# Attention over convolution projections: two halvings of v put off, transposes reordered at the image boundary, wider rows of v and a shifted k

## The chip, the cores and the metric

The kernel runs on one core of a Trainium2 chip. The metric is device time in microseconds, the median of several executions. "Span" is the time from the first to the last instruction of the one profiled execution. TensorE multiplies matrices; VectorE (DVE), ScalarE (ACT) and GpSimd (POOL) do the rest.

## The reference

Four images x of 64 x 64 x 256 in float32. Per image:

```python
q = einsum('bwhc,cd->bwhd', x, Wq) + bq      # 128 channels
k = einsum('bwhc,cd->bwhd', x, Wk) + bk      # 128 channels
v = einsum('bwhc,cd->bwhd', x, Wv) + bv      # 256 channels
pq, pk, pv = (t.reshape(B, -1, N) for t in (q, k, v))    # N = 4096
attention = softmax(einsum('bcn,bcm->bnm', pq, pk), axis=-1)
out = einsum('bcm,bnm->bcn', pv, attention)
return gamma * out.reshape(B, W, H, C) + x
```

## The kernel before

An image has two stages. In the first, 16 blocks of x are transposed, projected to q, k and v, and split into parts (h, l, d: "halving"). In the second, 128 units run: 16 groups of queries times 8 units of keys. A unit issues the energies of the unit three ahead, on TensorE, ScalarE takes exponentials, VectorE joins two of them, ScalarE and VectorE halve the product, and TensorE multiplies the halves of an earlier unit by the halves of v. The parts that matter:

```python
    vh = qkv.tile([P, NM, C + 2], F32R, tag="vh", name="vh")     # rows of 258 floats: 256 and two ones
    vl = qkv.tile([P, NM, C + 2], F32R, tag="vl", name="vl")
    vd = qkv.tile([P, NM, C], F32R, tag="vd", name="vd")
    # ... (cut)
    def project_v(b, i):
        images[b].v(i)
        v4 = now["v4"]
        m = slice(2 * i, 2 * i + 2)
        h = vh[:, m, :C]
        nc.scalar.activation(h, v4, AF.Identity, scale=UPPER * E)
        for t, f in ((vl, 1.0 / E), (vd, 1.0 / E + 1.0)):
            nc.vector.scalar_tensor_tensor(t[:, m, :C], h.bitcast(F32), -f, v4, ALU.mult, ALU.add)
    # energy(b, u, k): (cut)  weights are rows of k, the moving operand is q
        for to, f, first, last in ((sa, 0, True, False), (sa, 1, False, True), (sb, 2, True, True)):
            nc.tensor.matmul(to[:, i], kt[:, 2 * k + i, f, :], q[:, :, f, :], start=first, stop=last)
    # attend(b, u, j): (cut)  weights are h, l, d of the unit, the moving operand is a row of v
        for out_, left, right in ((a, h, vh), (a, l, vl), (bb[:, j, :], d, vd)):
            for i in range(4):
                nc.tensor.matmul(out_, left[:, i, n], right[:, m, :], ...)
    # the units of an image (cut)
        for u in range(STEPS):
            for k in range(2):
                if ahead < STEPS:
                    energy(b, ahead, k)
                if k == 0 and u + 2 < STEPS:
                    join(b, u + 2)
                    upper(b, u + 2)
            # ... (cut)
            halves(b, u + 1)
            # ... (cut)
            for j in range(NJ):
                attend(b, u, j)
        if b + 1 < B:
            images[b + 1].transposed(1)
            project_qk(b + 1, 0)
        while active:                  # the last output of the image
            proceed()
```

## Time and profile before

| | before |
|---|---|
| time | 2519.3 us (2519.1 to 2519.8, four runs) |
| TensorE busy | 2497.4 us, 99% of the span of 2516.5 |
| VectorE, ScalarE busy | 84%, 72% |
| granted clock of TensorE | 0.999 |

A TensorE that is busy for 99% of the span leaves two places to look: the 1%, and the pace of the matmuls within the 99%. The pace isn't in the durations, which overlap (282 ns is the mean of the sa matmuls of this trace), but in the starts. These two lines of the timeline of TensorE stand at the ends of the twelve energies of one unit in the steady stage (start us, duration us, instruction):

```profile
574.02 0.40 PE L311 MATMUL sa<-q,k 128*128 128x256 f32 x2
...
575.43 0.65 PE L359 MATMUL a<-vh,h 128*128 128x258 f32 x4
```

Twelve matmuls start in 1.41 us, 117.5 ns each, and this distance from start to start is the measure that the rest of the study uses.

### The profile page before, as it was taken

The numbers are of one execution on the slowest core, as the hardware profiler recorded it, in microseconds if no ns is written. First come the engines' busy times: TensorE is split into PE (matmuls) and PEld (weight loads), VectorE is DVE, ScalarE is ACT, GpSimd is POOL, SyncE is SP. The second block draws the span as 40 slices with busy tenths as digits, with TensorE's granted clock in tenths as the row PEclk, the third lists the DMA queues.
The fourth block names the chain that finished last, engine by engine and source line by source line (L and its number), as shares of the span: only waits on it lengthen the run. The fifth ranks groups of instructions, "written<-read, shape, count | busy, mean of one in ns | idle before, by whom it ended". The sixth has DMA issues, their size and how long they took to land.

```text
span 2516.5 us, 50017 instructions
## 1 busy us (share of the span) xinstructions
PE 2497.4 (99%) x19982; PEld 2455.1 (98%) x19982; DVE 2102.5 (84%) x2440; ACT 1806.1 (72%) x3138; POOL 424.6 (17%) x780
## 2 busy tenths in 40 slices
PE   9999999999999999999999999999999999999998
PEld 8999999999899999999989999999998999999998
DVE  5888888888688888888868888888886888888887
ACT  5777777776677777777667777777766777777775
POOL 4211111111411111111041111111114111111110
PEclk9999999999999999999999999999999999999999
DMA  7666666664766666666476666666648666666663
GB/s 238 214 192 210 198 203 197 193 207 147 236 214 189 206 198 201 201 191 205 138 243 220 194 192 207 200 206 194 190 143 254 213 197 195 201 200 206 198 191 108
DMA packets 137407, 498.92 MB, mean 198 GB/s; under 512 B 15536, under 2 KB 57264, under 8 KB 137168
## 3 DMA queue, kind: packets, MB, share of 16 engines
q0 software_dynamic: 92320, 453.17, 57.4%
q1 hardware_dynamic: 44304, 42.22, 5.6%
q8 instruction: 160, 2.62, 0.4%
q14 instruction: 79, 0.65, 0.1%
q10 hardware_dynamic: 544, 0.26, 0.0%
HBM read 445.25 MB, written 50.33 MB: 197 GB/s over the span
## 4 chain that ended last, share of the span: by engine, by line


## 5 line engine op out<-in xcount | busy, mean ns | idle before, releaser
L315 ACT ACTIVATE x<-sa 128x512 f32<-128x512 f32 x1024 | 609.5, 595 | 429.6 <-PE sa L311 367.6
L325 DVE TENSOR_TENSOR x<-x,y 128x1024 f32<-128x1024 f32 x512 | 625.4, 1222 | 172.9 <-ACT y L315 172.9
L311 PE MATMUL sa<-q,k 128*128 128x256 f32 x4096 | 759.2, 282 | 6.3 <-ACT x L315 6.0
L359 PE MATMUL a<-vh,h 128*128 128x258 f32 x4096 | 662.4, 284 | 0.0
L359 PE MATMUL a<-vl,l 128*128 128x258 f32 x4096 | 660.3, 283 | 0.0
L359 PE MATMUL bb<-vd,d 128*128 128x256 f32 x4096 | 651.9, 281 | 0.0
L311 PEld LDWEIGHTS sa<-q,k 128*128 128x128 f32 x4096 | 627.1, 188 | 8.0 <-ACT x L315 6.9
L336 DVE TENSOR_TENSOR l<-x,h 128x1024 fp32r<-128x1024 f32 x512 | 623.6, 1218 | 0.0
L339 DVE SCALAR_TENSOR_TENSOR d<-h,x 128x1024 fp32r<-128x1024 f32 x512 | 623.5, 1218 | 0.0
L315 ACT ACTIVATE y<-sb 128x512 f32<-128x512 f32 x1024 | 613.1, 599 | 0.0
L311 PE MATMUL sb<-q,k 128*128 128x256 f32 x2048 | 580.4, 283 | 0.0
L330 ACT ACTIVATE h<-x 128x1024 fp32r<-128x1024 f32 x512 | 543.5, 1061 | 34.9 <-DVE x L325 34.0
L359 PEld LDWEIGHTS a<-vl,l 128*128 128x128 f32 x4096 | 563.8, 189 | 0.0
L359 PEld LDWEIGHTS a<-vh,h 128*128 128x128 f32 x4096 | 561.5, 189 | 0.0
L359 PEld LDWEIGHTS bb<-vd,d 128*128 128x128 f32 x4096 | 557.6, 189 | 0.0
L295 POOL DMA_DIRECT2D k<-kf x512 | 279.7, 546 | 1508.1 <-PE sb L311 1476.0
L311 PEld LDWEIGHTS sb<-q,k 128*128 128x128 f32 x2048 | 385.4, 188 | 8.7 <-ACT y L315 0.8
L136 PE MATMUL qk<-wqk_sb,xts 128*128 128x256 f32 x512 | 121.5, 380 | 0.0
L157 PE MATMUL v<-xts,wv_sb 128*128 128x256 f32 x512 | 120.3, 379 | 0.0
L157 PEld LDWEIGHTS v<-xts,wv_sb 128*128 128x128 f32 x512 | 97.3, 190 | 13.2
L397 ACT ACTIVATE o<-o,r 128x256 f32<-128x256 f32 x126 | 57.4, 502 | 72.4 <-DVE r L380 72.4
L136 PEld LDWEIGHTS qk<-wqk_sb,xts 128*128 128x128 f32 x512 | 92.7, 191 | 10.1
(54 smaller groups left out, 884.5 us busy)
## 6 DMA issues: line engine op xcount, KB each, us to landing
k<-kf POOLq DMA_DIRECT2D x512, 768.0 KB, 4.8
x<-in_x_dram SPq DMA_DIRECT2D x128, 256.0 KB, 3.6
kf<-f POOLq DMA_DIRECT2D x64, 384.0 KB, 4.2
out_dram<-x POOLq DMA_DIRECT2D x63, 256.0 KB, 2.5
qd<-qks POOLq DMA_DIRECT2D x128, 64.0 KB, 2.9
qr<-qd SPq DMA_DIRECT2D x64, 128.0 KB, 3.1
wv_sb<-in_L_conv_Wv_dram POOLq DMA_DIRECT2D x1, 256.0 KB, 5.4
out_dram<-x SPq DMA_DIRECT2D x1, 256.0 KB, 3.9
```

The costliest lines, as they stand in the source:

```text
L136: nc.tensor.matmul(qk[:, s, :], self.xt[i][:, k, s, :], wqk_sb[:, k, :], start=(k == 0), stop=(k == KC - 1),)
L157: nc.tensor.matmul(vp[:, eh, :], wv_sb[:, k, eh * P : (eh + 1) * P], self.xt[i][:, k].rearrange("p s a -> p (s a)"), start=(k == 0), stop= ...
L295: nc.gpsimd.dma_start(t.rearrange("p (i s) f d -> p i s (f d)", s=2), kf[b, u % NU])
L311: nc.tensor.matmul(to[:, i], kt[:, 2 * k + i, f, :], q[:, :, f, :], start=first, stop=last)
L315: nc.scalar.activation(to[:, 2 * k : 2 * k + 2, :], sp.rearrange("p i j d -> p i (j d)"), AF.Exp, scale=scale,)
L325: nc.vector.tensor_tensor(x, x, y, ALU.mult)
L330: nc.scalar.activation(h, units[b, u], AF.Identity, scale=UPPER)
L336: nc.vector.tensor_tensor(l, x, h.bitcast(F32), ALU.subtract)
L339: nc.vector.scalar_tensor_tensor(d, h.bitcast(F32), 1.0 + E, x, ALU.mult, ALU.subtract)
L359: nc.tensor.matmul(out_, left[:, i, n], right[:, m, :], start=(t == i == 0 and (left is h or left is d and j == 0)), stop=(t == NU - 1 and ...
L397: nc.scalar.activation(o[:, j, :], o[:, j, :], AF.Identity, scale=r[:, j : j + 1])
```

## The change

Its intent: take work out of VectorE's queue where TensorE waits for it; let TensorE do the next image's transposes while the last output is scaled; and place two pairs of operands at other distances in memory. Nothing is computed differently. The core of the diff (cut; the guard's ok moves from its own 512 bytes to a y buffer, and ra into the tile of r, which frees the room):

```diff
+    VC = C + 4
-    ok = const.tile([P, B * NG * NJ], F32, name="ok")
-        vh = qkv.tile([P, NM, C + 2], F32R, tag="vh", name="vh")
-        vl = qkv.tile([P, NM, C + 2], F32R, tag="vl", name="vl")
+        vh = qkv.tile([P, NM, VC], F32R, tag="vh", name="vh")
+        vl = qkv.tile([P, NM, VC], F32R, tag="vl", name="vl")
@@ project_v
-            v4 = now["v4"]
+            units[b, "v4", i] = now["v4"]
+            if i < NI - 2:
+                halve_v(b, i)
@@ attend
-                        right[:, m, :],
+                        right[:, m, : out_.shape[1]],
@@ factors
-            r = work.tile([P, NJ], F32, tag="r", name=f"r_{b}_{g}")
+            r = work.tile([P, 2, NJ], F32, tag="r", name=f"r_{b}_{g}")
@@ finish_last
-            ra = work.tile([P, NJ], F32, tag="ra", name="ra", bufs=1)
@@ projections of the next image
                     pr.transposed(i + 1)
+                while i == 1 and active:
+                    proceed()
@@ units
+                if u in (1, 3):
+                    halve_v(b, NI - 2 + u // 2)
@@ end of an image
-            while active:
-                proceed()
```

More of the change, by code (lines that the diff above doesn't have):

```diff
@@ L209 @@
         ps_t = pool("ps_t", 1, space=PSUM)
-        vh = qkv.tile([P, NM, C + 2], F32R, tag="vh", name="vh")
-        vl = qkv.tile([P, NM, C + 2], F32R, tag="vl", name="vl")
+        vh = qkv.tile([P, NM, VC], F32R, tag="vh", name="vh")
+        vl = qkv.tile([P, NM, VC], F32R, tag="vl", name="vl")
         vd = qkv.tile([P, NM, C], F32R, tag="vd", name="vd")
         for t in (vh, vl):
-            nc.scalar.copy(t[:, :, C:], ones[:, : 2 * NM].rearrange("p (m t) -> p m t", t=2))
+            nc.scalar.copy(t[:, :, C : C + 2], ones[:, : 2 * NM].rearrange("p (m t) -> p m t", t=2))
         images, qd, kf, units, loads, now = [], {}, {}, {}, {}, {}
@@ L271, in project_v, with halve_v @@
             images[b].v(i)
-            v4 = now["v4"]
+            units[b, "v4", i] = now["v4"]
+            if i < NI - 2:
+                halve_v(b, i)
+        def halve_v(b, i):
+            v4 = units.pop((b, "v4", i))
             m = slice(2 * i, 2 * i + 2)
@@ L376, in factors @@
         def factors(b, g):
-            r = work.tile([P, NJ], F32, tag="r", name=f"r_{b}_{g}")
-            nc.vector.reciprocal(r, zall[:, b * NG + g, :])
-            nc.vector.tensor_tensor(r, r, gam.to_broadcast([P, NJ]), ALU.mult)
-            return r
+            r = work.tile([P, 2, NJ], F32, tag="r", name=f"r_{b}_{g}")
+            nc.vector.reciprocal(r[:, 0, :], zall[:, b * NG + g, :])
+            nc.vector.tensor_tensor(r[:, 0, :], r[:, 0, :], gam.to_broadcast([P, NJ]), ALU.mult)
+            return r[:, 0, :], r[:, 1, :]
         def whole(b, g):
@@ L394, in finish @@
             yield
-            r = factors(b, g)
+            r, _ = factors(b, g)
             for j in range(NJ):
@@ L414, in guard @@
             z = zall.rearrange("p n j -> p (n j)")
+            ok = ppool.tile([P, 4, NB], F32, tag="y", name="ok")[:, 0, : B * NG * NJ]
             nc.vector.tensor_scalar(ok, z, Z_LOW, None, ALU.is_ge)
@@ L429, in finish_last @@
             sums(b, g)
-            r = factors(b, g)
+            r, ra = factors(b, g)
             check = guard()
-            ra = work.tile([P, NJ], F32, tag="ra", name="ra", bufs=1)
             nc.vector.tensor_scalar(ra, r, 1.0 + E, None, ALU.mult)
```

## The prediction

> **What bounds the kernel now.** I read the page's head first: which engine is full, and at which clock.
>
> ```profile
> PE 2497.4 (99%) x19982; PEld 2455.1 (98%) x19982; DVE 2102.5 (84%) x2440; ACT 1806.1 (72%) x3138; POOL 424.6 (17%) x780
> PEclk9999999999999999999999999999999999999999
> ```
>
> TensorE is busy for 99% of the span at full clock. Nothing done on another engine can gain more than TensorE's own idle time plus any stretching of its matmuls. So I read the groups of instructions, for what fills it:
>
> ```profile
> L311 PE MATMUL sa<-q,k 128*128 128x256 f32 x4096 | 759.2, 282 | 6.3 <-ACT x L315 6.0
> L359 PE MATMUL a<-vh,h 128*128 128x258 f32 x4096 | 662.4, 284 | 0.0
> L359 PE MATMUL a<-vl,l 128*128 128x258 f32 x4096 | 660.3, 283 | 0.0
> L359 PE MATMUL bb<-vd,d 128*128 128x256 f32 x4096 | 651.9, 281 | 0.0
> ```
>
> Means of 281 to 284 ns are latencies of overlapping matmuls. What counts is the distance from one start to the next, which I took from the trace's start times (leaving out distances outside 100 to 140 ns, which are waits and changes of kind): 117.8 ns in the energies (sa and sb), 120.45 ns with vh, 120.55 with vl, 118.44 with vd. The 18432 such matmuls (6144 energies, 3 x 4096 for the output) make 6144 x 0.1178 + 4096 x (0.12045 + 0.12055 + 0.11844) = 2196 us, 87% of the span. Projections fill most of the rest, 216 ns for each of 1024 matmuls, 221 us.
>
> Then I searched the same start times for stalls of TensorE. The only repeated large one is at the second unit of each image. The timeline of TensorE there (second image):
>
> ```profile
> 703.29 0.40 PE L311 MATMUL sa<-q,k 128*128 128x256 f32 x2
> 703.53 0.28 PE L311 MATMUL sb<-q,k 128*128 128x256 f32 x1
> 703.64 0.40 PE L311 MATMUL sa<-q,k 128*128 128x256 f32 x2
> 703.88 0.28 PE L311 MATMUL sb<-q,k 128*128 128x256 f32 x1
> 705.71 0.50 PE L311 MATMUL sa<-q,k 128*128 128x256 f32 x2 [1.55 <-ACT x L315]
> 706.20 0.38 PE L311 MATMUL sb<-q,k 128*128 128x256 f32 x1
> ```
>
> The columns are start, duration, instruction, count, and in brackets idle time and its releaser. From 703.88 to 705.71 nothing starts, because the bank of sa is not read out yet. Why ScalarE is late, from its timeline and VectorE's:
>
> ```profile
> 701.13 0.59 ACT L315 ACTIVATE y<-sb 128x512 f32<-128x512 f32 x1
> 704.11 1.06 ACT L330 ACTIVATE h<-x 128x1024 fp32r<-128x1024 f32 x1 [2.39 <-DVE x L325]
> 705.08 0.58 ACT L315 ACTIVATE x<-sa 128x512 f32<-128x512 f32 x1
> ```
> ```profile
> 700.45 0.69 DVE L278 SCALAR_TENSOR_TENSOR vl<-vh,v 128x512 fp32r<-128x512 f32 x1
> 701.06 0.68 DVE L278 SCALAR_TENSOR_TENSOR vd<-vh,v 128x512 fp32r<-128x512 f32 x1
> 701.66 0.68 DVE L278 SCALAR_TENSOR_TENSOR vl<-vh,v 128x512 fp32r<-128x512 f32 x1
> 702.26 0.68 DVE L278 SCALAR_TENSOR_TENSOR vd<-vh,v 128x512 fp32r<-128x512 f32 x1
> 702.87 1.21 DVE L325 TENSOR_TENSOR x<-x,y 128x1024 f32<-128x1024 f32 x1
> ```
>
> VectorE halves the last two blocks of v (four operations, 700.45 to 702.87) before it joins x and y. ScalarE waits 2.39 us for that join, and the exponentials that free the bank stand behind it. The second place is the start of the next image:
>
> ```profile
> 631.42 1.89 PE L136 MATMUL qk<-wqk_sb,xts 128*128 128x256 f32 x8
> 633.48 0.95 PE L405 MATMUL ot<-ident,o 128*128 128x128 f32 x4 [0.17 <-ACT o L397]
> 634.26 0.60 PE L123 MATMUL xt<-ident,x 128*128 128x128 f32 x4
> ```
>
> The four transposes of the last output take 0.78 us to the next start, against 0.44 for those of x: they wait for the scaled o, before them and between them.
>
> [...] the exponentials had their inputs and stood behind h. [...] A row of 258 floats is 1032 bytes[...]. The trace speaks weakly: even rows are faster than odd ones for vl (119.58 against 121.53) and vh (120.13, 120.70), but also for vd (117.61, 119.26), whose rows of 1024 bytes are all aligned. [...]
>
> **The change part by part.**
> (1) Halving of v blocks 14 and 15 moves from before the first unit to the second and fourth (u = 1 and 3). Nothing is removed, only two ScalarE (0.63 us) and four VectorE operations (0.61 start to start) per image move to where VectorE has room. In the steady stage a unit is 4.28 us and VectorE's three operations are 3 x 1.135 = 3.41. With 2 x 0.61 it needs 4.63, 0.35 over. In unit 2 the halving of q (0.68) gives 4.09, 0.19 under. In unit 3 again 0.35 over. The join now starts some 0.67 us into a unit; it would start at most 0.5 us later than that at u = 4. In the profile the join was 3.4 us late (702.87 - 698.80 - 0.67) and the stall 1.7 plus slower restarts, so some 1.4 us of lateness are free: no new stall. ScalarE has 4 x 0.6 + 1.06 + 0.63 = 4.1 of 4.28. Blocks 14 and 15 are read only in units 6 and 7, so no wait there. Saved per image: the hole 1.71 plus 0.10 + 0.15 + 0.10 of restart in the second image (each distance less 118 ns); in the four images 2.1, 2.06, 2.1 and 2.0: 8.2 us, all on TensorE's path.
> (2) The third step's transposes of x go ahead of the last output's. ScalarE's second scaled o ends near 633.84. TensorE would be through with qk at 633.15 and x at 633.6, so the wait shrinks to about 0.2 us out of 0.62 (0.33 before, 0.29 within). 0.45 x 3 boundaries = 1.4 us. The x needed is loaded long before.
> (3) Rows of 260 floats. Columns multiplied stay 258. vh and vl now cost 120.5, vd 118.44; [...] 5 us.
> (4) k and q. From the memory map of the kernel before, k starts at 0 modulo 64 bytes and q at 32; modulo 512 they are 96 apart. Taking ok (512 bytes) and ra (32) out, and adding 2 x 256 for the wider rows, leaves q where it is and moves k down by 32 bytes: 64 apart modulo 512. [...] 5 us, as someone went to lengths for these 32 bytes but no row supports it.
> (5) r and ra in one tile, ok in a y buffer: the same operations; ok is used after the last join. Nothing.
> Sum: 2519.3 - 8.2 - 1.4 - 5 - 5 = 2499.7, say 2500 us.
>
> **The rivals.** First, the stall only moves: VectorE, 84% busy, falls behind in units 1 to 3 and TensorE waits at unit 2 or 4. For it: two units are 0.35 us over. Against: some 1.4 us of lateness are free. It would cost 1 us x 4 and leave 2504. Second, the addresses do nothing ([...] the same parity effect in aligned vd): 2519.3 - 9.6 = 2510. [...] Fourth, new offsets make conflicts: cells of single rows range from 115.8 to 129.2 ns with vl, so 1 ns more over all 14336 matmuls touched is possible, 14 us, 2524.
>
> **Range and chances.** The schedule's part (9.6) is rather sure to 2 us; the addresses carry the spread, from +5 to -30. So 2482 to 2511 in 8 of 10. Faster by over 2% means below 2469, 40 us out of the addresses alone: 0.05. Slower by over 2%: 0.01. Within: 0.94.
>
> **What would show it.** In TensorE's timeline of the second unit no hole over 0.5 us, and ScalarE's h no longer waiting 2 us for the join; at u = 2 to 4 no new idle TensorE. At the image start, x's transposes ahead of ot and ot within 0.6 us. Start-to-start distances: energies near 117, vh and vl near 120. I am wrong if the energies or the output matmuls move by over 2 ns either way, or if the stall reappears within the first units.

## The result, and the profile after

The changed kernel takes 2500.12 us (2499.04 to 2501.08, four runs, all fast), the ratio to before is 0.9924 with a 95% interval of 0.9906 to 0.9941. A ratio here is the mean time of one kernel's fast runs over that of the other's fast runs of the same rounds, so not quite the ratio of the medians. The forecast was 2500. A total that is right to 0.1 us does not make its terms right (below: it was luck), so each was tested by itself.

From the page of the changed kernel, the busy times and the groups of matmuls (the lines of the source have moved by five; columns as in the prediction):

```profile
PE 2483.7 (99%) x19982; PEld 2442.8 (98%) x19982; DVE 2103.2 (84%) x2440; ACT 1807.1 (72%) x3138; POOL 425.7 (17%) x780
...
L316 PE MATMUL sa<-q,k 128*128 128x256 f32 x4096 | 749.9, 281 | 0.3
L364 PE MATMUL a<-vh,h 128*128 128x258 f32 x4096 | 661.2, 283 | 0.0
L364 PE MATMUL a<-vl,l 128*128 128x258 f32 x4096 | 658.2, 283 | 0.0
L364 PE MATMUL bb<-vd,d 128*128 128x256 f32 x4096 | 654.3, 282 | 0.0
```

The same numbers of instructions, and the same work on the other engines; the idle time ahead of sa has gone from 6.3 to 0.3 us. Of the outputs, vh and vl shrank by 1.2 and 2.1 us and vd grew by 2.4. Only sa shrank clearly.

The second unit of the second image, on TensorE, where the hole was:

```profile
697.40 0.40 PE L316 MATMUL sa<-q,k 128*128 128x256 f32 x2
697.64 0.28 PE L316 MATMUL sb<-q,k 128*128 128x256 f32 x1
697.76 0.40 PE L316 MATMUL sa<-q,k 128*128 128x256 f32 x2
697.99 0.28 PE L316 MATMUL sb<-q,k 128*128 128x256 f32 x1
698.11 0.40 PE L316 MATMUL sa<-q,k 128*128 128x256 f32 x2
```

The fifth line starts 0.12 us after the fourth; before, the distance was 1.83 us. The image boundary, TensorE:

```profile
626.61 1.89 PE L136 MATMUL qk<-wqk_sb,xts 128*128 128x256 f32 x8
628.34 0.60 PE L123 MATMUL xt<-ident,x 128*128 128x128 f32 x4
628.78 0.85 PE L410 MATMUL ot<-ident,o 128*128 128x128 f32 x4
629.54 1.99 PE L136 MATMUL qk<-wqk_sb,xts 128*128 128x256 f32 x8
...
629.54 1.59 PEld L136 LDWEIGHTS qk<-wqk_sb,xts 128*128 128x128 f32 x8 [0.15 <-ACT xts L129]
```

From the start of one projection of q and k to the start of the next it is now 629.54 - 626.61 = 2.93 us. Before it was 3.28 (631.42 to 634.70). Within ot a wait of some 0.19 us is left, about what was foreseen, but ot still takes 0.76 us to the next start, where 0.6 was. And something new stands behind it: the weights of that projection (the last line, PEld is TensorE's weight load) wait for ScalarE's copy of xts, and from its first matmul to its second it takes 0.32 us in place of 0.22. So 0.25 of the 0.35 us are kept.

There is a new small hole four units on, in the sixth unit. TensorE, then ScalarE, then VectorE, all of the changed kernel:

```profile
714.86 0.39 PE L316 MATMUL sa<-q,k 128*128 128x256 f32 x2
715.09 0.28 PE L316 MATMUL sb<-q,k 128*128 128x256 f32 x1
715.44 0.50 PE L316 MATMUL sa<-q,k 128*128 128x256 f32 x2
715.92 0.39 PE L316 MATMUL sb<-q,k 128*128 128x256 f32 x1
```
```profile
713.84 1.06 ACT L335 ACTIVATE h<-x 128x1024 fp32r<-128x1024 f32 x1 [1.58 <-DVE x L330]
714.81 0.58 ACT L320 ACTIVATE x<-sa 128x512 f32<-128x512 f32 x1
```
```profile
711.32 0.69 DVE L283 SCALAR_TENSOR_TENSOR vl<-vh,v 128x512 fp32r<-128x512 f32 x1 [0.41 <-ACT vh L280]
711.92 0.69 DVE L283 SCALAR_TENSOR_TENSOR vd<-vh,v 128x512 fp32r<-128x512 f32 x1
712.53 1.22 DVE L330 TENSOR_TENSOR x<-x,y 128x1024 f32<-128x1024 f32 x1
```

It is the old stall in small: VectorE's join waits behind the second put-off halving, ScalarE's h waits 1.58 us for the join, and the exponential that frees a bank stands behind h. The bracket on the first VectorE line shows what the prediction had left out: VectorE sat idle for 0.41 us until ScalarE had made vh, which stood in ScalarE's own queue. The join belongs to the fifth unit (u = 4), whose energies started at 710.22, so it came at +2.31 us where +0.67 is usual: 1.6 us late, not 0.5. The prediction put the free lateness at 1.4 us, and the excess shows in the sixth unit as 0.23 + 0.14 us, or 0.59 with two slower restarts of 0.10 each, counted as the prediction counted the old hole.

Last, the energies. A unit of the changed kernel, and another three units on, on TensorE:

```profile
889.09 0.39 PE L316 MATMUL sa<-q,k 128*128 128x256 f32 x2
...
890.45 0.41 PE L364 MATMUL a<-vh,h 128*128 128x258 f32 x2
```
```profile
901.81 0.40 PE L316 MATMUL sa<-q,k 128*128 128x256 f32 x2
...
903.22 0.46 PE L364 MATMUL a<-vh,h 128*128 128x258 f32 x2
```

The first takes 1.36 us for its twelve energies, 113.4 ns each, the second 1.41 us as before. From the start times of all units, averaged over the groups of an image but the first two, by the place of the energies' unit in its group: 113.4, 113.4, 113.4, 117.8, 115.7, 117.8, 118.0, 118.0 ns. Before, all eight places lie between 117.2 and 118.9. So some units run at another pace, and the same places in every group; only the fifth varies from group to group.

These means leave out distances of 160 ns and more, and so hide a stall that the prediction's search passed over. In all groups but the first of each image, the fifth place follows the transposes of a finished output. One such unit of the changed kernel, TensorE, then ScalarE:

```profile
802.92 0.39 PE L316 MATMUL sa<-q,k 128*128 128x256 f32 x2
803.23 0.39 PE L316 MATMUL sb<-q,k 128*128 128x256 f32 x1
803.45 0.40 PE L316 MATMUL sa<-q,k 128*128 128x256 f32 x2
```
```profile
799.38 0.92 ACT L402 ACTIVATE o<-o,r 128x256 f32<-128x256 f32 x2 [1.15 <-DVE r L385]
...
801.15 1.05 ACT L335 ACTIVATE h<-x 128x1024 fp32r<-128x1024 f32 x1
802.10 0.59 ACT L320 ACTIVATE x<-sa 128x512 f32<-128x512 f32 x1
802.58 0.60 ACT L320 ACTIVATE y<-sb 128x512 f32<-128x512 f32 x1
```

TensorE's sb at 803.23 waits until ScalarE has read the bank of sb (802.58 + 0.60), which stands behind the scaled o and h in ScalarE's queue (the first groups, with no output to scale, have no such wait). With the slower restart this costs 0.19 us in each of 60 groups; from the first energy after the transposes to the second it takes another 0.09 us longer than usual. Together that is 16.3 us, against 16.5 before: twice the hole that the change removed, and no run of this study touches it.

### The profile page after: what moved, and what is told of

Same layout as the page of the kernel before. It is cut to its first block, busy times and chain, and to the rows that moved or that the text cites. A ratio compares the mean times of both kernels' runs of the same rounds, so it can differ in the third digit from the quotient of the medians.

```text
span 2497.3 us, 50025 instructions
## 1 busy us (share of the span) xinstructions
PE 2483.7 (99%) x19982; PEld 2442.8 (98%) x19982; DVE 2103.2 (84%) x2440; ACT 1807.1 (72%) x3138; POOL 425.7 (17%) x780
## 4 chain that ended last, share of the span: by engine, by line
PE 97%; ACT 2%; DVE 1%; issue 0%; DMA 0%; SPq 0%; ACTq 0%; DVEq 0%
PE a L364 38%; PE bb L364 19%; PE sa L316 19%; PE sb L316 10%; PE qk L136 4%; PE v L157 4%; PE ot L410 1%; PE xt L123 1%; ACT h L335 1%; DVE x L330 1%; ACT x L320 0%; ACT y L320 0%; DVE vd L283 0%; DMA x<-in_x_dram 0%; ACT vh L280 0%
## 5 line engine op out<-in xcount | busy, mean ns | idle before, releaser
L316 PE MATMUL sa<-q,k 128*128 128x256 f32 x4096 | 749.9, 281 | 0.3
L157 PE MATMUL v<-xts,wv_sb 128*128 128x256 f32 x512 | 120.3, 379 | 0.0
```

Of the source, the lines that this page charges most:

```text
L157: nc.tensor.matmul(vp[:, eh, :], wv_sb[:, k, eh * P : (eh + 1) * P], self.xt[i][:, k].rearrange("p s a -> p (s a)"), start=(k == 0), stop= ...
```

## The experiments

To keep the noise of the start of the program out (see the last section), I cut every trace from the first energy matmul to the last output matmul and added up the distances from each start to the next. A distance of 160 ns or more after an energy is counted as 118 ns of work and the rest as a wait. "Outputs" are the matmuls with vh, vl and vd, waits included; "rest" is projections and transposes after the first energy. The kernel that was traced twice (e7 and e12) has sums of 2438.4 and 2439.2. All in us:

| kernel | k from q | row of v | energies | waits at energies | outputs | rest | sum |
|---|---|---|---|---|---|---|---|
| before | 96 | 258 | 723.7 | 29.0 | 1475.5 | 232.4 | 2460.6 |
| changed | 64 | 260 | 713.8 | 22.3 | 1473.8 | 231.6 | 2441.6 |
| e1, k alone | 64 | 258 | 709.1 | 29.8 | 1475.5 | 232.3 | 2446.7 |
| e2, rows alone | 96 | 260 | 725.9 | 28.9 | 1473.6 | 232.4 | 2460.7 |
| e3, halving alone | 96 | 258 | 723.7 | 22.7 | 1474.4 | 232.4 | 2453.2 |
| e4, order alone | 96 | 258 | 723.7 | 28.4 | 1475.8 | 231.6 | 2459.6 |
| e5, changed, narrow rows | 64 | 258 | 709.3 | 23.2 | 1475.7 | 231.6 | 2439.8 |
| e8, changed, k at 0 | 0 | 260 | 734.4 | 20.2 | 1474.3 | 231.6 | 2460.5 |
| e11, changed, k at 32 | 32 | 260 | 726.3 | 22.6 | 1471.7 | 231.6 | 2452.1 |
| e6, changed, k at 128 | 128 | 260 | 729.1 | 22.1 | 1470.1 | 231.6 | 2452.9 |
| e7, changed, d 64 from vd | 64 | 260 | 714.3 | 24.4 | 1468.2 | 231.6 | 2438.4 |
| e10, changed, halving in units 2 and 5 | 64 | 260 | 713.5 | 20.2 | 1473.8 | 231.6 | 2439.0 |
| e9, three at once | 64 | 258 | 716.8 | 22.8 | 1472.7 | 231.6 | 2443.9 |

"k from q" is the distance in bytes modulo 512 (both tiles step in multiples of 512 bytes from buffer to buffer and row to row, so it is the same for all pairs).

My theory after seeing the result: the distance of k from q gives more than its 5 us and the rows of v give no time. Rivals: the rows make the quick units; or the new order does.

**e1: k alone.** Only ra is put into the tile of r, in the kernel before.

```diff
-            r = work.tile([P, NJ], F32, tag="r", name=f"r_{b}_{g}")
+            r = work.tile([P, 2, NJ], F32, tag="r", name=f"r_{b}_{g}")
-            ra = work.tile([P, NJ], F32, tag="ra", name="ra", bufs=1)
```

> Before with one thing changed: ra lies in the tile of r, so k and f lie 32 bytes lower and k is 64 bytes from q (modulo 512) where it was 96; the operations, their order and the rows of v are as before. If the distance of k from q sets the time of the energies' weight loads (my theory): the distance of one energy matmul to the next falls from 117.8 to about 116.1 ns as in the changed kernel, with a part of the units at 113.4, and the time falls by about 10 us, to 2509. If it is the rows or the order of work that brought the 113.4 ns units: no change, 2519.

Measured: 2505.86 us, ratio 0.9947 (0.9930 to 0.9963). Thirty-two bytes, and 13.9 us less between the first energy and the last output; the energies alone give 14.6. Four of the eight places are at 113.4 to 113.8 ns and two at 115.5 to 115.9. The rivals fall: neither wide rows nor the new order are needed.

**e2: rows alone.** Rows of 260 floats in the kernel before, k left at 96.

```diff
+    VC = C + 4
-        vh = qkv.tile([P, NM, C + 2], F32R, tag="vh", name="vh")
+        vh = qkv.tile([P, NM, VC], F32R, tag="vh", name="vh")
```

> Before with rows of 260 floats for vh and vl (and ok in a y buffer to make room); k stays 96 bytes from q. If alignment of rows to 16 bytes matters (the step of the prediction): vh and vl fall by about 0.6 ns each, 5 us, 2514. If it does not: start-to-start of vh and vl stays within 0.3 ns of 120.5 and the time within 3 us of 2519.

Measured: 2520.74 us, ratio 1.0004 (0.9995 to 1.0012): no gain in time. Outputs take 1.9 us less, energies 2.2 more. By kind (distances of 100 to 140 ns from each start to the next) vh falls from 120.6 to 119.6 ns and vl from 120.55 to 120.3, on average the 0.6 ns of the first expectation; but energies rise from 117.8 to 118.15 and vd from 118.4 to 118.65, although by the memory maps neither operand of these has moved. In the kernel before every second row (of 1032 bytes) starts at an address that is no multiple of 16 bytes, here (1040 bytes) none does, and the twelve timed runs show no gain. (This trace holds 3.4 us at half clock, see the last section; its distances of over 150 ns there add up to 1.5 us, which stand in the sum but not in the means by kind.)

**e3: halving alone.** The kernel before with halve_v put off to the second and fourth unit.

> Before with the halving of v blocks 14 and 15 put off to the second and fourth unit, nothing else. Theory: the hole of 1.7 us in the second unit goes in all four images, 8.2 us, 2511, and no new one comes. Rival: the stall moves on to unit 2 or 4 and less than half of that is gained, 2515 or more.

Measured: 2513.24 us, ratio 0.9971 (0.9961 to 0.9982), 7.5 us less between the two marks. The hole of 1.7 us is gone in all images; small ones of 0.17 to 0.20 and 0.14 to 0.15 us, with restarts of some 0.10 after each, stand in the sixth unit. Both halves of the expectation hold in part: most is gained, a little is given back.

**e4: order alone.** The kernel before with the last output behind the third step's transposes.

> Before with the third step's transposes of x ahead of the last output's. Theory: 0.4 us at each of three boundaries, 1.3 us, 2518. Rival: the later scaled output or the load of x makes it nothing or worse, 2519.3 or more.

Measured: 2518.97 us, ratio 0.9996 (0.9988 to 1.0005). The time can't tell this from nothing. The trace can: rest falls by 0.8 us, and the boundary above is 0.35 us shorter, of which 0.10 is lost just behind it, three times. This trace also holds something else, windows of the second image (stretch, its length, then busy us and count on TensorE, weight loads, VectorE, ScalarE and GpSimd, then the granted clock, the DMA share and GB/s):

```profile
704.00:707.40 3.40, 1.85 (x13) 1.46 (x13) 3.40 (x4) 2.22 (x4) 0.00 (x0) 1.00 0.96 360
707.60:710.80 3.20, 3.20 (x17) 3.20 (x17) 3.20 (x4) 2.72 (x5) 0.53 (x1) 0.50 0.49 121
```

The hole of the second unit (TensorE is busy for 1.85 of 3.40 us) was followed by 3.4 us at half clock, in which the outputs start some 214 ns apart; some 1.5 us of this kernel's outputs in the table are that. More on this in the last section.

**e5: the changed kernel with narrow rows.** VC is C + 2 and ok is back in its own tile, so that q and k stay where they are.

> The changed kernel with rows of 258 floats again; k stays 64 from q and the order of work stays changed. If the parts add up (k alone 0.53% of before, putting off the halving 0.29%, the order 0.04%), the ratio to before is 0.9914 against 0.9924 for the whole change: about 2497.5 where before has 2519.3; the wide rows then cost rather than gain, because with them only three of the eight units of a group have energies at 113.4 ns. If wide rows help once the rest is there: 2503 or more.

Measured: 2499.18 us, ratio 0.9918 (0.9905 to 0.9932), against 0.9924 for the change. The intervals overlap, so the times don't decide; the sums do in one trace each: 1.7 us less. Energies fall by 4.5 us to the level of e1, outputs rise by 1.9. So wide rows gain no time even where k is 64 from q. They change which units are quick (mean of the energies 116.1 ns with them, 115.35 without), and by kind it is as in e2: with them vh is 0.9 and vl 0.3 ns faster, vd 1.0 slower.

**e6, e8, e11: k at 128, 0 and 32.** Only small tiles between q and k change size or place. For e6:

```diff
-            r = work.tile([P, 2, NJ], F32, tag="r", name=f"r_{b}_{g}")
+            r = work.tile([P, 8, NJ], F32, tag="r", name=f"r_{b}_{g}")
```

For e8, r lies in a fixed tile ahead of everything, which also moves q and all tiles of v by 32 bytes; for e11, r has one buffer where it had two.

> The changed kernel with 64 bytes more between q and k: 128 bytes from q. If what counts is the distance modulo 64: energies as with 64, a part of the units at 113.4 ns, mean near 116. If it is a window that only some distances hit: no unit at 113.4, mean near 118, and 5 to 10 us slower than the changed kernel.

> The changed kernel with r in its own fixed tile, so that k is 0 bytes from q modulo 512. If the distance counts modulo 64: as with 64, mean of the energies near 116 ns. If equal addresses collide: above 118 ns, slower than the changed kernel by 10 us or more.

> The changed kernel with one buffer of r where there were two, so that k is 32 bytes from q. If only the neighbourhood of 64 is good (0 gave 119.6 ns, 96 some 118, 128 gave 118.5): between 118 and 119.6 ns, no unit at 113.4, about 2512. If the good window reaches down to 32: near 116 ns and 2500.

Measured (one run each, so of unknown state, at a granted clock of 0.998 to 0.999): 2512.51, 2520.74 and 2510.55 us. None has a quick unit: the means of the eight places lie in 118.4 to 119.2 ns (128), 119.0 to 120.0 (0) and 117.8 to 119.0 (32). The energies' sums are 729.1, 734.4 and 726.3 us against 713.8 at 64. So 64 is a window, not a rule modulo 64 or 32, and 0 is the worst of those tried, 20.6 us over 64. The same unit as above in e8, TensorE:

```profile
898.06 0.40 PE L317 MATMUL sa<-q,k 128*128 128x256 f32 x2
...
899.49 0.28 PE L365 MATMUL a<-vh,h 128*128 128x258 f32 x1
```

1.43 us for twelve: 119.2 ns each.

**e7 and e12: d 64 from vd.** If 64 is good for k and q, it may be for d and vd, which are at 0.

```diff
         vd = qkv.tile([P, NM, C], F32R, tag="vd", name="vd")
+        pad = qkv.tile([P, 16], F32, tag="pad", name="pad")
+        nc.vector.memset(pad, 0.0)
```

The pad moves h, l and d together, and q and k with them: h and l also come to stand 64 bytes further from vh and vl, and k stays 64 from q.

> The changed kernel with 64 bytes between vd and the buffers of h, l and d, so that d is 64 from vd (modulo 512) where it was 0; k stays 64 from q. If 64 bytes between weights and moving rows is what makes a weight load quick: vd falls from 119 towards 114 ns, 15 to 20 us faster. If it is particular to the energies: vd within 0.7 ns of 119.

> The kernel with 64 bytes between vd and d once more, now timed: if its single time of 2496.5 was no accident, ratio to before about 0.9907, against 0.9924 for the changed kernel; if it was, 0.992 or more.

Measured: 2496.51 us once, then 2498.15 (four runs), ratio 0.9909 (0.9894 to 0.9924). The distance from one vd matmul to the next falls from 118.99 to 117.7 ns, not to 114: neither expectation of e7 holds. vh falls from 120.0 to 119.3 and vl rises from 120.0 to 120.25, so the run doesn't show which of the three moves did it. Outputs fall by 5.6 us, waits rise by 2.1, and 3.2 us are gained in the first trace and 2.4 in the second. This is the best median ratio of the study, but its interval overlaps that of the changed kernel, so it is not shown to beat it.

**e10: halving in the second and fifth unit.**

```diff
-                if u in (1, 3):
-                    halve_v(b, NI - 2 + u // 2)
+                if u in (1, 4):
+                    halve_v(b, NI - 2 + u // 3)
```

> The changed kernel with block 15 of v halved in the fifth unit where it was in the fourth. If VectorE's backlog of two halvings and q's within three units makes the new small holes of the sixth unit (0.23 and 0.14 us): they go, 0.3 us in each image, 1.2 us in all, 2499. If they have another cause they stay.

Measured: 2498.98 us, ratio 0.9914 (0.9901 to 0.9928). The sixth unit of the second image, TensorE, at the place of the hole:

```profile
716.79 0.39 PE L316 MATMUL sa<-q,k 128*128 128x256 f32 x2
717.02 0.28 PE L316 MATMUL sb<-q,k 128*128 128x256 f32 x1
717.13 0.39 PE L316 MATMUL sa<-q,k 128*128 128x256 f32 x2
```

The third line starts 0.11 us after the second: the hole is gone, and the waits at energies fall by 2.1 us. VectorE's backlog was the cause of the hole. The interval of the time overlaps that of the changed kernel.

**e9: three at once.** Narrow rows, d 64 from vd, and the halving of e10.

> A version meant to beat both: the changed kernel with rows of 258 floats, 64 bytes between vd and the buffers of h, l and d, and the second halving of v in the fifth unit where it was in the fourth. If the three gains add: 1 us from the rows, 3.5 from the distance of d from vd, 1.5 from the stall in the sixth unit, about 2494, ratio to before 0.990. If the distances between weight loads and rows work only in the setting they were found in, it is at 2500 or over.

Measured: 2502.13 us, ratio 0.9928 (0.9914 to 0.9941): not better than the change. The gains don't add. vd falls to 117.3 ns, but of the energies only the first place is still near 113.3 and five are at 117.5 to 117.7.

**What stays open.** Within one kernel, with the same distances for all units, whole units run at 113.4 ns and others at 118, by their place in the group; and rows of v, which the energies don't read, decide which (e5 against the changed kernel). So the distance of k from q alone does not set the pace. In the changed kernel's fifth place the pace even changes within a unit: 114 to 115 ns from its third matmul to the stall, 116 to 118 after it (means of 56 groups). In the start times of the changed kernel each weight load starts 3 to 4 ns after a matmul, and its own matmul follows 110 ns later in quick units and 114 to 115 in slow ones. What makes that distance longer, no run shows. By the memory maps q, h, l and d stand at the same place modulo 512 in every kernel here, so that "64 from q" is also 64 from these three; that it is q is argued from q being the operand that the energies read. What the runs rule out is k's own address: in e6 and e7 k stands at 416 modulo 512, and only in e7, where q has moved along, is the mean of the energies 116.2 ns; in e6 it is 118.7.

## Why the prediction was right

The time, 2500.12, is the 2500 predicted, and it was within the range of 2482 to 2511. What bounds the kernel and the stall were understood; that the total came out exact was luck in two other terms. By steps:

1. *What bounds it.* Right. All that was gained is TensorE's: waits at energies and the distance between starts. Work on other engines is unchanged.
2. *The stall (8.2 us).* Right in mechanism. The hole is gone from the trace, and the part alone gave 7.5 us (e3). "No new stall" was slightly wrong: the sum of VectorE's work left out its waits for ScalarE's vh (0.35 and 0.41 us idle), the join came 1.6 us late in place of 0.5, and a hole of 0.59 us per image with its restarts, 2.4 us in all, came back in the sixth unit, one later than the prediction looked for it. e10 confirms it by removing it. This is the first rival, at a smaller size than it was given.
3. *The order of transposes (1.4 us).* Right in kind: the waits before and within ot fell by 0.43 us at each of three boundaries, where 0.45 was foreseen. What was left out is that the next projection then waits itself, 0.18 us around its first matmul, so that 0.25 a boundary, 0.8 us, are kept. The timed runs alone would not have shown it.
4. *Rows of 260 floats (5 us).* Wrong. Alone they gain no time (e2), and in the changed kernel they cost 1.7 us by one trace each (e5). vh and vl did fall, by 0.65 ns on average in e2, near the 0.6 ns that the expectation of e2 names for 5 us; the 5 us themselves were the author's estimate. What failed is the step that all else keeps its pace: energies and vd, whose addresses stayed, grew slower, by more than half of that gain in e2 and by more than all of it in the changed kernel. That alignment moved vh and vl isn't shown either: the prediction itself held the counter-evidence, that vd, whose rows of 1024 bytes all start at multiples of 16, shows such a difference of even and odd rows too (117.61 against 119.26 ns from each start to the next).
5. *k 64 from q (5 us).* The kind was right, the size two to three times too small: 13.9 us alone (e1), 9.9 in the energies of the changed kernel, where the wide rows take a part back. The 5 us had no row to support them and were the author's estimate; only the runs give the size.

Terms 4 and 5 were 10 together, and together the runs gave about 10.5 (19.0 for the whole less 7.5 of e3 and 1.0 of e4). In the changed kernel waits at energies fell by 6.7 and rest by 0.8, energies by 9.9 and outputs by 1.7, which make the 19.0 of the two sums. The total is right because two wrong terms cancel, which is luck, and the third and fourth rivals (addresses that do much, faster in the third and slower in the fourth) were nearer to the truth than the central case: between the best and the worst distance of k tried, all else of the changed kernel kept, lie 20.6 us of the energies. (The 120.45 ns of vh comes out as 120.6 by the prediction's own rule, and the 120.13 of its even rows as 120.57. Neither changes the forecast.)

Of the signs that it named, the hole in the second unit is gone, energies at 116.1 and vh and vl at 120.0 ns are near what it said, and no kind moved by over 2 ns; but ot takes 0.76 us and not 0.6, and some of the eight places moved by over 4 ns, which a mean of all energies hides.

## What to carry to other kernels

When an engine is 99% busy, add up the distances from start to start by kind of instruction: a pace that is 4% off is worth more here than every hole: all 6144 energies at 113.4 ns in place of 117.8 would save 27 us, by an estimate from these two figures. Where matmuls each load new weights, vary the distance in memory between weights and moving operand in small steps (here 32 bytes) and look at the distance between starts: of the five distances tried here 64 was the best (116.1 ns on average in the changed kernel) and 0, equal addresses modulo 512, the worst (119.6 in e8). Measure again when neighbouring matmuls change, for the gains of e5, e7 and e10 did not add in e9. When work is put off to fill another engine's slack, count its waits for its inputs, not only its own durations. And look for short stalls that repeat: 0.27 us in each of 60 groups is more than 2 us in each of four images.

## What the traces and runs show beyond this kernel's schedule

- The pace of the energies (matmuls of 256 columns) goes with the distance of the weights from the moving operand: 116.1 ns on average at 64 bytes (113.4 in the best units), 118.2 at 32, 118.7 at 128, 119.6 at 0 (the changed kernel, e11, e6, e8).
- In the changed kernel an energy matmul starts 110 ns after the start of its weight load in the best units and 114 to 115 in others, and no unit of any trace has a mean below 113 ns from start to start. Whether a unit can be quicker than that, no run shows.
- Rows of 1040 bytes in place of 1032 for the moving operands vh and vl gave no gain in time: ratio 1.0004 (e2).
- In e4 a hole of 1.55 us of idle TensorE was followed by 3.4 us at half clock (0.50 in the window above), and in e2's trace the same length stands behind the hole of the first image (83.5 to 86.9 us). Two of the sixteen such holes in the four traces that have them (before, e1, e2, e4) were followed by a dip; what decides it isn't shown. None of the ten traces without the hole has a dip between the first 15 us and the end of the program.
- The start of the program differs between executions of one kernel. The kernel of e7 and e12 is the same; full clock came 6.1 us after the first instruction in e7's trace and 13.8 us in e12's, where a projection of eight matmuls at 8.71 us took 3.62 us (1.89 at a granted clock of 1.00, at 626.61 in the changed kernel's trace). The spans are 2494.6 and 2498.6, and 3.2 of these 4.0 us lie ahead of the first energy (at 45.1 and 48.3 us). What sets the moment of full clock isn't shown.
